# Early normalisation of images 1 to 3, softmax reciprocals by DMA a block later, and 5x5 convolutions without identity products

## The chip, the cores and the metric

The kernel runs on one core of one Trainium2 chip. The metric is the device time of one launch in microseconds (us). The core has five engines that run their own instruction streams in order: PE (TensorE, matrix products), DVE (VectorE), ACT (ScalarE), POOL (GpSimd) and SP (SyncE, which here does nothing but issue DMAs). An instruction waits on semaphores for what it needs, and everything behind it on the same engine waits with it.

## The reference, cut to what matters

Four layers, each with a residual, on `x` of shape (4, 128, 64, 64): four images of 128 channels and L = 4096 pixels. All is float32. `_gn` is a group norm over 4 channels at a time.

```
x = x + attention(_gn(x))     # q, k, v by 128x128 matrices; softmax over 4096 x 4096 scores
x = x + conv5x5(_gn(x))       # weights built from two small tables
x = x + scan(_gn(x))          # state-space scan, 64 states, forward and backward halves
x = x + conv3x3(_gn(x))
```

The scan's recurrence over 4096 pixels, for 128 channels and 64 states, is the largest piece of elementwise work; attention is the largest piece of products.

## The kernel before, in words

**The tiling.** Channels lie on the 128 partitions. A block of attention is 512 queries (`MM`), so an image has 8 blocks (`NM`), and a block has 32 units (`NJT`) of 128 keys. In unit `u`, PE makes a product of scores into PSUM, ACT takes its exponential into a ring of 8 slots, and two units later (`w = u - 2`) PE multiplies the slot by the values into the bank `acc`. The softmax denominators are sums over the keys. In image 0 they are added up beside, by DVE and POOL in turn, into two tiles (`side_sums`, L531 to L541). In images 1 to 3 PE makes them: once in four units, four products with a matrix of ones into the four column groups of bank `z` (`sums`, L511 to L524).

**The end of a block.** When the last unit of a block is through, `evict_sums` and `evict` copy sums and values out of PSUM (ACT). Then `attention` queues four steps for the units that follow (L624 to L625): `turn` one unit later (PE: small products that put the sums of 512 queries on partitions), `invert` two later (DVE: copy and reciprocal), `widen_out` four later (PE: `spread`, four 128-column products with the identity that lay the reciprocals along a row on all partitions), `settle` five later (DVE: multiply and add to the residual; ACT: a square for the next group norm).

**The 5x5 convolution** (`conv_pairs`, L837) treats rows in pairs, four chunks an image. In images 1 to 3 (`lean`) a chunk has three groups: a shared part of 10 products in bank `s`, copied to SBUF by ACT (`q`), and 15 products for the even and the odd rows (banks `a`, `z`), each closed with a product of the identity and `q` (L996), so that the shared part is added on PE. Image 0 has another grouping, which the change leaves as it is.

**The scan** is a loop of 1024 ticks (`scan_core`), 256 an image. A tick has one multiplication on POOL (`drive`, L1268), the decays on ACT (L1261), the recurrence on DVE (L1278), a multiplication on DVE (L1281) or POOL (`weigh`, L1299) as `to_pool` deals them out, and small products on PE (`collect`, L1317). SP loads one pair of broadcast rows (`br`, `cr`, L1239) in every second tick, four ticks ahead (`AHEAD`), into three buffers each.

**The order of the work** is written out by hand. All other work of the kernel is one generator, `images()`: `front(0)` to `front(3)` (attention, 5x5 convolution, then the operands of the scan), then the ends of all images (back projection, 3x3 convolution). Each `yield` names a price in estimated PE microseconds: 0.86 for a product (`PRODUCT`), 1.7 for a hop to another engine (`HOP`), 0.7 for a slot of the operands (`SLOT`). Image 0's front runs alone, ahead of the scan. From then on each tick of the scan earns 2.8 of credit (`PACE`; 1.5 in the last image, `ENDPACE`), and as much of the generator is issued between the tick's instructions as the credit pays for (L1583 to L1593). So the front of image b + 1 is spread over the 256 ticks of image b. If the scan's next image is due (four ticks ahead) and its first operands aren't there, `before` (L1567) issues the generator without ticks until they are.

**The operands** (`scan_operands`, L1034) are 60-odd slots of short steps on all engines. Beside them, image b + 1 begins: `start` (L1414) loads the image, `attention_start` (L396) takes its statistics (8 `bn_stats` on DVE, L401), makes the group norm (some 15 small DVE and POOL instructions, `group_norm`, L349), normalises on ACT (L392) and makes the values.

Of the kernel before, what the change touches and what calls it, by code (L numbers as in the profile page):

```python
# [24 lines left out]
F32 = mybir.dt.float32  # L25
I32 = mybir.dt.int32
AF = mybir.ActivationFunctionType
ALU = mybir.AluOpType
# [4 lines left out]
P = 128  # L33
GROUPS = 32
GN_EPS = 1e-5
CH = 1024
# [6 lines left out]

PRODUCT, HOP, SLOT, PACE, ENDPACE, AHEAD = 0.86, 1.7, 0.7, 2.8, 1.5, 4


BQ, BK, BX, BP, CONVB, BD, DSKIP, MAINB, CONVW, ALOG = 0, 1, 2, 3, 4, 5, 6, 7, 8, 12
# [3 lines left out]
def conv_preact_kernel(  # L53
# [340 lines left out]

    def attention_start(b, xn):

        st = stats_tile(f"a{b}")
        for i in range(NM):  # L400
            nc.vector.bn_stats(st[:, i, :], xn[:, bass.ts(i, MM)])  # L401
            yield 0.0
        gn = yield from group_norm(st, f"a{b}")
        while b > 0 and (b - 1, "taps") not in ready:
            yield 0.0
        v = pools["big"].tile([P, VSIZE], F32, tag="V", name=f"v_{b}")
        v = v[:, : NJT * C].rearrange("p (j c) -> p j c", c=C)
        pvs = {}

        def piece(i):  # L410
            cut = bass.ts(i, L // 4)
            normalise(xn[:, cut], xn[:, cut], gn)

        def keys(i):

            tag = "saz"[i % 3] if b == 0 else "s" if i < 3 else ("s", "s2")[i % 2]
            pvs[i] = bank(tag, f"pv_{b}_{i}").rearrange("p (t c) -> p t c", c=C)
            for t in range(TPM):
                nc.tensor.matmul(
                    pvs[i][:, t, :], xn[:, bass.ts(i * TPM + t, P)], wv, start=True, stop=True  # L420
                )

        def take(i):
            nc.scalar.copy(v[:, i * TPM : (i + 1) * TPM, :], pvs.pop(i))

        piece(0)
        yield SLOT
        for i in range(NM):
            if i % 2 == 0 and i // 2 + 1 < 4:
                piece(i // 2 + 1)  # L430
            keys(i)
            yield SLOT
            if b > 0:
                take(i)
                yield 0.0
            elif i > 0:
                take(i - 1)
        if b == 0:
            take(NM - 1)
        return xn, v  # L440

    def attention(b, xs, xn, v, st, safe, loads):
# [15 lines left out]
        def row_max(blk):  # L458

            part = small.tile([P, TPM, NM], F32, tag="part", name=f"part_{b}_{blk}")  # L460
            for t in range(TPM):
                for k in range(NM):
                    pp = bank("s", f"pmax_{b}_{blk}_{t}_{k}")
                    nc.tensor.matmul(
                        pp, rq[blk][:, bass.ts(t, P)], xn[:, bass.ts(k, MM)],
                        start=True, stop=True,
                    )
                    nc.vector.tensor_reduce(part[:, t, k : k + 1], pp, AX.X, ALU.max)
            m = small.tile([P, TPM], F32, tag="rmax", name=f"rmax_{b}_{blk}")
            nc.vector.tensor_reduce(m, part, AX.X, ALU.max)  # L470
            pb = bank("s", f"pmb_{b}_{blk}")
            spread(pb, m)
            mb[blk] = pools["bg"].tile([P, MM], F32, tag="w", bufs=4, name=f"mb_{b}_{blk}")
            nc.scalar.copy(mb[blk], pb)

        def spread(dst, cols):
# [66 lines left out]
        def evict_sums(blk):  # L543
            zs = None
            if not fill:
                zs = pools["bg"].tile([P, MM], F32, tag="zs", bufs=1, name=f"zs_{b}_{blk}")
                nc.scalar.copy(zs, zp.pop(blk))
            state[blk] = None, zs

        def evict(blk):  # L550
            raw = pools["bg"].tile([P, MM], F32, tag="raw", bufs=1, name=f"raw_{b}_{blk}")
            nc.scalar.copy(raw, acc.pop(blk))  # L552
            state[blk] = raw, state[blk][1]

# [43 lines left out]
        for u in range(N):  # L598
# [11 lines left out]
            if w >= 0:  # L610
                if w < N - HELD:
                    values(w)
                    cost += PRODUCT
                d = w % NJT
                if fill:
                    side_sums(w)
                elif d == NJT - 1:
                    sums(w)
                    cost += PRODUCT
                elif d % 4 == 3:  # L620
                    due.append((w, u + (3 if d == 3 else 1), u + NRING - 5))
                if d == NJT - 1:
                    evict_sums(blk - 1)
                    evict(blk - 1)  # L624
                    for n, f in ((1, turn), (2, invert), (4, widen_out), (5, settle)):  # L625
                        after(u, n, f, blk - 1)
            for f, args in later.pop(u, ()):
                f(*args)
                cost += PRODUCT if f in (turn, widen_out) else 0.0
            next(loads, None)  # L630
            yield cost or HOP
        for w in (N - 2, N - 1) if fill else ():
# [9 lines left out]
                nc.sync.dma_start(to[:, : part.shape[1], :], part)  # L642

        values(N - 4)
        yield PRODUCT
        while due:
            sums(due.pop(0)[0])
            yield PRODUCT
        for n in range(NRING - 4):
            taps_to(n)  # L650
        if not fill:
# [183 lines left out]
    def conv_pairs(b, xs, tag, st, st2, lean):  # L835
# [86 lines left out]
        piece(1)  # L922
        differences(0)
        K5 = 5
        steps, done = [], None
        taps5 = more[0] if wide else exchange(b)[:, : NTAP * C].rearrange("p (k c) -> p k c", c=C)

        def matrix(w, dx):
# [11 lines left out]
            )  # L940
            st2.squares(i, chunk(xs, c, y), xs[:, 0:1])

        for c in range(L // CH):
            j = c * CK
            if c < 2:
                piece(2 + c)
            if c < 3:
                differences(c + 1)
            accs = [
                (bank("s", f"pq_{b}_{c}"), ((SUM12, image, 2 * j + 2), (SUM34, image, 2 * j + 4))),  # L950
                (bank("a", f"pe0_{b}_{c}"),
                 ((0, image, 2 * j), (1, diff, j), (3, diff, j + 1))),
                (bank("z", f"pe1_{b}_{c}"),
                 ((0, image, 2 * j + 1), (2, diff, NP + j + 1), (4, diff, NP + j + 2))),
            ]
            if wide:
                total, first, last = (combo(n) for n in range(3))
                accs = [
                    (accs[0][0], (accs[0][1][1], (HSUM, total, j))),
                    (bank("y", f"pm_{b}_{c}"), ((HDIF, diff, j),)),  # L960
                    (accs[1][0], ((0, first, j), (3, diff, j + 1))),
                    (accs[2][0], ((2, last, j), (4, diff, NP + j + 2))),
                ]
            for n, (acc, parts) in enumerate(accs):
                k, total = 0, len(parts) * K5
                for w, view, r in parts:
                    for dx in range(K5):
                        k += 1
                        nc.tensor.matmul(  # L969
                            flat(acc), matrix(w, dx), view(r, dx),  # L970
                            start=k == 1, stop=k == total and (n == 0 or not lean),
                        )
                        if k == 3 and done is not None:
                            done()
                            done = None
                        if k % 3 == 0:
                            yield 3 * PRODUCT
                if n == 0:
                    qs = pools["bg"].tile([P, MM], F32, tag="w", bufs=4, name=f"q_{b}_{c}")

                    def done(acc=acc, qs=qs, c=c):
                        nc.scalar.copy(qs, acc)
                        for y in range(0 if lean else 2):
                            nc.gpsimd.tensor_tensor(
                                chunk(xs, c, y), chunk(xs, c, y), flat(qs), ALU.add
                            )
                    yield PRODUCT
                elif wide and n == 1:
                    def done(acc=acc, c=c):
                        for y, op in enumerate((ALU.subtract, ALU.add)):  # L990
                            nc.vector.tensor_tensor(
                                chunk(xs, c, y), chunk(xs, c, y), flat(acc), op
                            )
                else:
                    if lean:
                        nc.tensor.matmul(acc, ident, qs, start=False, stop=True)  # L996
                        yield PRODUCT

                    def done(acc=acc, c=c, y=n - len(accs) + 2):
                        add(c, y, acc)  # L1000
        yield HOP
# [399 lines left out]
    def program(safe):  # L1401
# [4 lines left out]
        if safe:  # L1406
            nc.sync.dma_start(cs[:, :10, :], kept_sums)

        def load(tile, b):
            for c in range(NCH):  # L1410
                nc.sync.dma_start(tile[:, bass.ts(c, CH)], xf[b][:, bass.ts(c, CH)])
                yield 0.0

        def start(b, after=0):  # L1414
# [3 lines left out]
            for _ in range(after):  # L1418
                yield 0.0
            xn = large(b, f"x_{b}")[:, :L]  # L1420
            yield from load(xn, b)
            for _ in range(after):
                yield 0.0
            return (yield from attention_start(b, xn))
# [1 line left out]
        def front(b, xn, v):  # L1426

            xs = large(b + 1, f"xs_{b}")[:, :L]
            st = Sums(f"e{b}")
            yield from attention(b, xs, xn, v, st, safe, load(xs, b))  # L1430
            st2 = Sums(f"s{b}")

            yield from conv_pairs(b, xs, f"A{b % 2}", st, st2, b > 0 or safe)
# [86 lines left out]
        with ExitStack() as es, tc.manual_schedule():  # L1520
# [26 lines left out]
            if not safe:  # L1547
                with tc.tile_pool(name="fill", bufs=2) as pools["fill"]:
# [7 lines left out]
                    with tc.tile_pool(name="tables", bufs=1) as tmp:  # L1556
                        for _ in chain(scan_constants(), build_conv_weights(tmp, more[0]), more_weights(*more)):
                            for _ in range(4):
                                next(work)
                    while (0, "convolved") not in ready:  # L1560
                        next(work)
                del pools["fill"]
# [112 lines left out]
```

## Time and profile before

| | |
|---|---|
| median of 3 runs | 4425.56 us (4419.15 to 4431.18) |
| the profiled execution's own time | 4426.94 us |
| its span, first to last instruction | 4425.1 us |
| PE busy, instructions | 3896.3 us (88%), 13352 |
| DVE busy | 3702.6 us (84%), 3471 |
| POOL busy | 3603.6 us (81%), 1713 |
| ACT busy | 2377.4 us (54%), 4301 |
| mean granted PE clock | 0.936 |
| DMA | 726.05 MB, mean 164 GB/s |

The shares are means over unlike stages. Up to 684 us image 0's front runs alone; then the scan's ticks run to 4355 us, in the first three images with the next image's front between them, in the last with the ends of the images. So every stage has its own bound, and is read by itself.

### The profile page before, as it was taken

The numbers are of one execution on the slowest core, as the hardware profiler recorded it, in microseconds if no ns is written. First come the engines' busy times: TensorE is split into PE (matmuls) and PEld (weight loads), VectorE is DVE, ScalarE is ACT, GpSimd is POOL, SyncE is SP. The second block draws the span as 40 slices with busy tenths as digits, with TensorE's granted clock in tenths as the row PEclk, the third lists the DMA queues.
The fourth block names the chain that finished last, engine by engine and source line by source line (L and its number), as shares of the span: only waits on it lengthen the run. The fifth ranks groups of instructions, "written<-read, shape, count | busy, mean of one in ns | idle before, by whom it ended". The sixth has DMA issues, their size and how long they took to land. (4 is left out here: it accounts for less than half of the span.)

```text
span 4425.1 us, 42907 instructions
## 1 busy us (share of the span) xinstructions
PE 3896.3 (88%) x13352; PEld 1486.0 (34%) x13352; DVE 3702.6 (84%) x3471; ACT 2377.4 (54%) x4301; POOL 3603.6 (81%) x1713
## 2 busy tenths in 40 slices
PE   8999997999999979999989889999989657575667
PEld 4444433333333323333333333333333112121212
DVE  4722217999999989999999889999999899999996
ACT  3333217666665376666664576666643754444533
POOL 3433307999999968999989889999999789999995
PEclk9999999999999989999999989999999868787888
DMA  1000016545555565544545564555555666656562
GB/s 64 21 1 1 0 53 231 185 167 176 177 176 182 176 238 198 176 176 168 185 173 181 201 228 168 175 177 175 176 181 177 223 221 206 228 195 232 187 227 84
DMA packets 216302, 726.05 MB, mean 164 GB/s; under 512 B 26240, under 2 KB 27520, under 8 KB 215808
## 3 DMA queue, kind: packets, MB, share of 16 engines
q1 hardware_dynamic: 214144, 722.49, 47.1%
q8 instruction: 107, 1.75, 0.2%
q14 instruction: 131, 1.07, 0.1%
q10 hardware_dynamic: 1920, 0.73, 0.1%
HBM read 653.98 MB, written 69.14 MB: 163 GB/s over the span
## 5 line engine op out<-in xcount | busy, mean ns | idle before, releaser
L1268 POOL TENSOR_TENSOR db<-dx,br 128x1024 f32<-128x1024 f32 x1024 | 2399.5, 2366 | 224.8 <-DMA dx<-dxd 76.7
L1261 ACT ACTIVATE da<-de,a_neg 128x512 f32<-128x512 f32 (+1 forms) x1640 | 1303.1, 797 | 759.6 <-DVE da L1278 305.0
L487 PE MATMUL sc<-r,x 128*128 128x512 f32 x2048 | 1082.2, 611 | 22.5 <-ACT last L1294 9.7
L499 PE MATMUL acc<-exchange,v 128*128 128x512 f32 x2048 | 1048.6, 594 | 2.7 <-ACT raw L552 0.5
L1299 POOL TENSOR_TENSOR hc<-hc,cr 128x1024 f32<-128x1024 f32 x386 | 913.3, 2366 | 22.9 <-ACT last L1294 20.9
L1281 DVE TENSOR_TENSOR hc<-da,cr 128x512 f32<-128x512 f32 (+1 forms) x1003 | 839.5, 837 | 65.7 <-issue 1.3
L1278 DVE TENSOR_TENSOR_SCAN da<-da,last,db 128x512 f32<-128x512 f32 (+1 forms) x480 | 863.1, 1798 | 22.6 <-POOL db L1268 17.7
L493 ACT ACTIVATE exchange<-sc 128x512 f32<-128x512 f32 x1024 | 603.6, 589 | 503.1 <-PE sc L487 494.6
L1317 PE MATMUL y<-hc,sel 128*32 128x512 f32 x4096 | 604.8, 650 | 284.4 <-POOL hc L1299 230.9
L487 PEld LDWEIGHTS sc<-r,x 128*128 128x128 f32 x2048 | 361.8, 190 | 596.5 <-issue 376.7
L499 PEld LDWEIGHTS acc<-exchange,v 128*128 128x128 f32 x2048 | 386.9, 190 | 500.6 <-issue 478.5
L1278 DVE TENSOR_TENSOR_SCAN hc<-da,last,db 128x512 f32<-128x512 f32 (+1 forms) x288 | 490.9, 1705 | 6.4 <-ACT da L1261 3.3
L1278 DVE TENSOR_TENSOR_SCAN da<-da,da,db 128x512 f32<-128x512 f32 x365 | 469.7, 1287 | 6.8 <-ACT da L1261 6.6
L541 POOL TENSOR_TENSOR sidep<-sidep,exchange 128x512 f32<-128x512 f32 x120 | 170.8, 1423 | 273.4 <-ACT exchange L493 271.1
L1317 PEld LDWEIGHTS y<-hc,sel 128*32 128x32 f32 x4096 | 114.4, 113 | 715.5 <-POOL hc L1299 315.2
L1278 DVE TENSOR_TENSOR_SCAN hc<-da,hc,db 128x512 f32<-128x512 f32 x251 | 322.0, 1283 | 32.7 <-ACT da L1261 8.9
L541 DVE TENSOR_TENSOR sided<-sided,exchange 128x512 f32<-128x512 f32 x120 | 95.9, 799 | 221.7 <-ACT exchange L493 220.3
L1278 DVE TENSOR_TENSOR_SCAN da<-da,db 128x512 f32<-128x512 f32 (+1 forms) x158 | 232.4, 1471 | 13.1 <-ACT da L1261 10.1
L703 PE MATMUL pcm<-xpm,cs 128*128 128x512 f32 x432 | 214.5, 646 | 25.2 <-ACT xpm L392 25.2
L969 PE MATMUL pe<-df,exchange 128*128 128x512 f32 x480 | 214.2, 595 | 0.0
L521 PE MATMUL zp<-exchange,ones 128*32 128x512 f32 x1536 | 205.3, 601 | 9.6 <-DVE xs L588 9.5
L1294 ACT COPY last<-da 128x1 f32<-128x1 f32 x474 | 73.8, 156 | 259.7 <-DVE hc L1281 257.2
(239 smaller groups left out, 2838.8 us busy)
## 6 DMA issues: line engine op xcount, KB each, us to landing
br<-bm SPq DMA_DIRECT2D x512, 512.0 KB, 5.2
cr<-cm SPq DMA_DIRECT2D x512, 512.0 KB, 4.0
de<-dd SPq DMA_DIRECT2D x64, 512.0 KB, 4.9
dx<-dxd SPq DMA_DIRECT2D x64, 512.0 KB, 6.2
x<-in_x_dram SPq DMA_DIRECT2D x16, 512.0 KB, 6.0
xs<-in_x_dram SPq DMA_DIRECT2D x16, 512.0 KB, 6.6
xsd<-xs SPq DMA_DIRECT2D x16, 512.0 KB, 6.8
xcd<-xc SPq DMA_DIRECT2D x16, 512.0 KB, 2.9
```

What stands on the lines that cost most here:

```text
L487: nc.tensor.matmul(sc, xn[:, bass.ts(j, P)], rq[blk], start=True, stop=True)
L493: nc.scalar.activation(pt, sc, AF.Exp)
L499: nc.tensor.matmul(acc[blk], v[:, j, :], ring[:, u % NRING, :], start=j == 0, stop=j == NJT - 1)
L541: eng.tensor_tensor(s, s, ring[:, u % NRING, :], ALU.add)
L703: nc.tensor.matmul(acc.rearrange("p (r w) -> p r w", w=W), weights[:, t, :], xp[:, y : y + RPM, dx : dx + W], start=t == 0, stop=t == k * ...
L969: nc.tensor.matmul(flat(acc), matrix(w, dx), view(r, dx), start=k == 1, stop=k == total and (n == 0 or not lean),)
L1261: nc.scalar.activation(da, rep["de", b, c, d, g][:, bass.ts(h, size)], AF.Exp, scale=a_neg[:, at(i)])
L1268: nc.gpsimd.tensor_tensor(dbs[i], rep["dx", b, c, d, g], rows["b", b, c, d, q], ALU.mult)
L1278: nc.vector.tensor_tensor_scan(h, da, db[:, cut], before, ALU.mult, ALU.add)
L1281: nc.vector.tensor_tensor(hc[:, cut], h, rows["c", b, c, d, q][:, cut], ALU.mult)
L1299: nc.gpsimd.tensor_tensor(hcs[i], hcs[i], rows["c", b, c, d, q], ALU.mult)
L1317: nc.tensor.matmul(y[r : r + SG, :], sel, hcs[first + gg][:, bass.ts(h, MM)], start=False, stop=q == NQ - 1, tile_position=(0, r), skip_gr ...
```

## The change

Four things change.

1. `normalise_ahead` runs in image 0's front, after the weights of the convolutions are built: it loads images 1 to 3, takes their statistics, normalises them and stores them to DRAM (`normed`). `start` then loads the normalised image, and `attention_start` makes no statistics, group norm or normalisation for images 1 to 3. The residual is still loaded from `x`.
2. `turn`, `invert`, `widen_out` go, but for the last block of an image. In their place, `spill` stores the sums to DRAM (2 units after the block), `gather` loads them with the queries on partitions (4), `invert_rows` adds the parts and takes the reciprocal on DVE (7), `put_rows` stores it (9) and `fetch_rows` loads it as a row on all partitions (11). At the end of the *next* block ACT copies that row into bank `z` (`stage_rows`), and `settle` follows a unit later. In image 0, two products with ones add up the side sums over the partitions first.
3. In the `lean` convolution ACT copies the shared part from its PSUM bank to a second one (`part`), and both groups of 15 go on adding to it in place. The products with the identity go. The order is shared part of chunk c, odd rows of chunk c - 1, even rows of chunk c; the shared parts alternate between banks `s` and `z`.
4. `PACE` is 2.74.

```diff
-PRODUCT, HOP, SLOT, PACE, ENDPACE, AHEAD = 0.86, 1.7, 0.7, 2.8, 1.5, 4
+PRODUCT, HOP, SLOT, PACE, ENDPACE, AHEAD = 0.86, 1.7, 0.7, 2.74, 1.5, 4
...
+    def normalise_ahead(pool):
+        for b in range(1, B):
+            t = pool.tile([P, L], F32, tag="ahead", name=f"ahead_{b}")
+            for c in range(NCH):
+                nc.sync.dma_start(t[:, bass.ts(c, CH)], xf[b][:, bass.ts(c, CH)])
+            st = stats_tile(f"a{b}")
+            for i in range(NM):
+                if i % 4 == 0:
+                    yield HOP
+                nc.vector.bn_stats(st[:, i, :], t[:, bass.ts(i, MM)])
+            yield HOP
+            gn = yield from group_norm(st, f"a{b}")
+            for c in range(NCH):
+                cut = bass.ts(c, CH)
+                normalise(t[:, cut], t[:, cut], gn)
+                nc.sync.dma_start(normed[b][:, cut], t[:, cut])
+                yield HOP
...
+            elif blk + 1 < NM:
+                zs = pools["bg"].tile([P, MM], F32, tag="zs", bufs=1, name=f"zs_{b}_{blk}")
+                pz = bank("z", f"pz_{b}_{blk}")
+                for g, e in enumerate("dp"):
+                    nc.tensor.matmul(
+                        pz[g * 32 : (g + 1) * 32, :], ones[:, :32], sides.pop((blk, e)),
+                        start=True, stop=True, tile_position=(0, g * 32), skip_group_check=True,
+                    )
+                nc.scalar.copy(zs[:64], pz[:64])
...
+        def spill(blk):
+            nc.sync.dma_start(zd[:n], zs[0 : n * 32 : 32, :])
...
+        def gather(blk):
+            nc.sync.dma_start(zt[:, :n, :], zd.rearrange("g (p j) -> p g j", j=RUN))
...
+        def invert_rows(blk):
+            nc.vector.tensor_reduce(z, zt.rearrange("p g j -> p j g"), AX.X, ALU.add)
+            nc.vector.reciprocal(zr, z)
...
+        def put_rows(blk):
+            nc.sync.dma_start(zd, zr)
...
+        def fetch_rows(blk):
+            row = zd.rearrange("p j -> (p j)").unsqueeze(0)
+            nc.sync.dma_start(rb, row.to_broadcast([P, MM]))
...
+        def stage_rows(blk, tag):
+            pb = bank(tag, f"rz_{b}_{blk}")
+            nc.scalar.copy(pb, rb)
...
-                    for n, f in ((1, turn), (2, invert), (4, widen_out), (5, settle)):
+                    for n, f in (
+                        (2, spill), (4, gather), (7, invert_rows), (9, put_rows), (11, fetch_rows)
+                    ):
                         after(u, n, f, blk - 1)
+                    if blk > 1:
+                        stage_rows(blk - 2, "z")
+                        after(u, 1, settle, blk - 2)
...
+        for c in range(NCK + 1 if lean else 0):
+            if c < NCK:
+                advance(c)
+                yield from shared_of(c)
+                done = lambda c=c: part(c)
+            if c > 0:
+                yield from second_of(c - 1)
+            else:
+                yield HOP
+                done()
+                done = None
+            if c < NCK:
+                yield from first_of(c)
...
+                    with tc.tile_pool(name="norm", bufs=1) as tmp:
+                        for _ in normalise_ahead(tmp):
+                            for _ in range(3):
+                                next(work)
```

`shared_of` is the group of 10 products, `second_of` and `first_of` those of 15, opened without clearing the bank; `part(c)` is `nc.scalar.copy(owns[c], held[c])`. A step given as `done` is issued after the third product of the group that follows.

## The prediction

> **What bounds the kernel now.** I read the page's totals first, then the busy times by stage, then the groups of instructions, then who waits for whom. The totals do not decide: three engines are over 80% busy.
>
> ```profile
> span 4425.1 us, 42907 instructions
> PE 3896.3 (88%) x13352; PEld 1486.0 (34%) x13352; DVE 3702.6 (84%) x3471; ACT 2377.4 (54%) x4301; POOL 3603.6 (81%) x1713
> ```
>
> So I cut the span at the stages that the groups' first and last starts show. Columns: window; its length and PE's busy time; then PEld, DVE, ACT, POOL, each with a count; granted PE clock; DMA share; GB/s.
>
> ```profile
> 30.00:500.00 470.00, 468.16 (x1233) 217.53 (x1232) 182.80 (x234) 167.67 (x286) 176.34 (x131) 1.00 0.01 5
> 730.00:1364.00 634.00, 621.54 (x2377) 232.96 (x2377) 602.68 (x618) 413.04 (x851) 598.62 (x259) 1.00 0.52 180
> 1380.00:1554.00 174.00, 173.95 (x543) 68.77 (x544) 163.46 (x101) 72.10 (x81) 168.76 (x78) 0.98 0.51 171
> 1554.00:1661.00 107.00, 78.29 (x313) 30.41 (x311) 87.96 (x114) 83.78 (x138) 73.36 (x39) 0.86 0.67 235
> 1600.00:1610.00 10.00, 10.00 (x40) 3.13 (x38) 6.94 (x11) 8.71 (x15) 0.00 (x0) 1.00 0.38 147
> 1630.00:1650.00 20.00, 14.89 (x80) 9.78 (x80) 17.67 (x20) 19.91 (x34) 15.27 (x7) 0.91 0.77 254
> 3540.00:4351.00 811.00, 514.92 (x1587) 153.79 (x1591) 779.84 (x461) 382.29 (x605) 769.09 (x350) 0.78 0.62 213
> ```
>
> The reader is to see: image 0's attention (30 to 500) is PE's alone. Image 1's attention (730 to 1364) is PE at 98%, with DVE at 95% and POOL at 94% close behind. Its convolution (1380 to 1554) is PE at 100%, POOL at 97%, DVE at 94%. In the operands (1554 to 1661) no engine is full on the mean, ACT is for a while (19.91 of 20), and POOL stands still for 10 us. Images 2 and 3 repeat this (attention 639 and 638 us). The last image (from 3540) is DVE's and POOL's.
>
> ```profile
> L401 DVE BATCH_NORM_STATS2 st_a<-x 128x6 f32<-128x512 f32 x32 | 20.6, 682 | 7.1 <-DMA x<-in_x_dram 7.1
> L392 ACT ACTIVATE x<-x,nb_a,rs_a 128x1024 f32<-128x1024 f32 x16 | 19.8, 1241 | 1.8 <-POOL nb_a L387 1.8
> L996 PE MATMUL pe<-q,ident 128*128 128x512 f32 x48 | 25.1, 605 | 0.0
> L479 PE MATMUL pzb<-ident,zr 128*128 128x128 f32 x256 | 33.9, 275 | 1.6 <-DVE zr L575 1.6
> L564 PE MATMUL pz<-zsel,zs 128*128 128x1 f32 x192 | 22.8, 240 | 0.0
> L521 PE MATMUL zp<-exchange,ones 128*32 128x512 f32 x1536 | 205.3, 601 | 9.6 <-DVE xs L588 9.5
> ```
>
> PE's ends are modelled and overlap, so I price products by the distance of starts. In the timeline of a block's end:
>
> ```profile
> 1903.66 0.95 PE L564 MATMUL pz<-zsel,zs 128*128 128x1 f32 x8
> ...
> 1904.54 1.92 PE L1317 MATMUL y<-hc,sel 128*32 128x512 f32 x16
> ...
> 1911.65 1.05 PE L479 MATMUL pzb<-ident,zr 128*128 128x128 f32 x8
> ...
> 1912.54 1.02 PE L487 MATMUL sc<-r,x 128*128 128x512 f32 x2
> ```
>
> A turn takes 0.88 us of PE, a widening 0.89, a 512-column product 0.86 (two passes of 0.43). SP's own waits name what it stands for:
>
> ```profile
> SPq L1239 <- POOL hc L1299: 1463.1, 342, 19.1
> SPq L1239 <- DVE hc L1281: 841.1, 277, 10.6
> ```
>
> SP is idle most of the time, waiting for a row buffer to come free.
>
> **What the Trainium skill says.** (1) Perfetto Trace Analysis, "Identifying the Most-Contended Engine": matmul busy time says little of how near TensorE is to its best. The trace agrees that it flatters (0.95 busy for 0.88 of time), so I count starts. (2) TensorEngine Tiling (Array Packing), "Key Properties": tiles of the array work independently. The trace agrees: four 32-column products of L521 fill 0.99 us (1900.44 to 1901.43), hardly more than one whole product. (3) The same page, "Instruction Overhead": a product with one column costs as much as one with 60. The trace agrees in kind: the 16 passes of one column with which image 0 turns its sums take 1.7 us (88.52 to 90.22). (4) DMA: Bandwidth & Descriptors, "Two DMAs through the same engine are not ordered": a DMA that reads what another wrote has to be held until the first one's semaphore. Before, SP shows few such waits (three for `dxd`, 4.3 us in all); the change adds two a block.
>
> **The change part by part.** The sum is made against the profiled execution's own 4426.94 us (its span plus 1.8 us around it), 1.4 us above the median of the runs.
>
> *Image 0's end of block.* Its turn costs 88.44 to 90.22 = 1.78 us, its widening 0.89 (95.46 to 96.35); 7 blocks x 2.67 = 18.7 us of PE go. Two products with ones come, in two column groups: at most two whole products, 1.72, at least one, 0.86; by L521 I take 1.0, so 7.0. The sums are now copied out ahead of the values: the ones' product ends 1.0 after the block, two ACT copies of 0.59 and their hand-over follow, and PE wants the bank `acc` again after a 0.86 score product: some 0.65 us of wait x 7 = 4.5. The POOL sum that the ones' product waits for follows its exponential at once and is about 2 us early. Net -7.
>
> *Normalising ahead.* DVE 24 statistics (16 us), three group norms (10), ACT 12 x 1.24 = 15, POOL 6 small ones, SP 12 loads and 12 stores. They fall in 30 to 500, where DVE is 39%, ACT 36%, POOL 38% and DMA 1% busy. What is queued behind: DVE's side sums and ACT's exponentials. A load waits on SP for the store of the image before, so DVE may stand up to 5 us; the ring of 8 slots gives PE 6 units of 1.72 = 10 us. I take +1 (0 to +6). If the cover failed, PE would wait for exponentials. Stage in sum: -6 (-14 to 0).
>
> *Attention of images 1 to 3.* 7 x (0.88 + 0.89) = 12.4 us of PE go per image. PE also no longer waits for `settle` to free bank `z`: 9.5/3 = 3.2. So up to -15.6. But DVE's work here stays (603 us: a reduction and a reciprocal for a copy and a reciprocal), and with 619 us in place of 634 it would be 97% busy; the best stretches of the page's slices have 98%. I take -11 (-4 to -15.6). Ticks don't change in number: credit of attention before 592 products x 0.86 + 1.7 = 511, /2.8 = 182; after, without 14 of them, 499/2.74 = 182.
>
> *Convolution.* 8 identity products x 0.86 = 6.9 us of PE go per image. ACT's copy stays a copy (PSUM to PSUM instead of SBUF), 15 products ahead of its first user. In credit the convolution loses 4 x 2.58 - 1.7 = 8.6. With attention's 12.0 and the 1.7 of the hop in the group norm that is 22.3. By the ticks' starts the operands of image 1 begin at tick 248, 248 x 2.8 = 694; after, 672/2.74 = tick 245.3. They are due at tick 252 and need 34 slots x 0.7 + 2 hops = 27 of credit, so before 17 are issued without ticks, after 9: the stretch in which POOL stands still (1600 to 1610) is halved, and this is how POOL, at 97% in the convolution, can profit. I take -7 (-3 to -10).
>
> *Operands.* Gone from beside them, for each of images 1 to 3: DVE 8 x 0.65 = 5.2 and some 3.3 of group norm, ACT 4 x 1.24 = 5.0, POOL two small ones. In 1630 to 1650 ACT is full, and four normalisations are in it or next to it. The load has the same size. I take -5 (-2 to -9).
>
> *The DMAs by SP.* Per block four small DMAs and one of 256 KB written on chip, all on SP's queue, behind which the row loads stand, and behind those POOL's `drive`. Issue is about 0.5 us each. Spill waits for ACT's copy; gather for spill's landing (the 128 KB store of `ys` lands in 3.1 us), two units, 5 us, later; invert on DVE for gather, 7.5 us after; put for invert; fetch for put's landing. Rows have room: the `br` issued at 1906.24 is used at 1918.29; the median of issue to use is 10.9 us in that stretch, of landing 5.2, so 5.7 to spare. SP comes to a load about 6 us before DVE comes to the same place in the program, so it will stand for put and gather some 2 to 4 us, within the room. ACT's staging copy adds 0.59 per block where ACT is 65% busy. I take +1.5 per image (0 to +6).
>
> *Sum.* -6 + 3 x (-11 - 7 - 5 + 1.5) = -6 - 64.5 = -70.5; 4426.9 - 70.5 = **4356 us**. The last image, 811 us, is untouched.
>
> **The rivals.**
>
> *A: DVE and POOL become the bound at once.* For: 95% and 94% in attention, 97% in the convolution. Against: both reach 96 to 98% in the last image. Attention -4, convolution -2, operands -5, DMAs +1.5: -6 - 3 x 9.5 = -34.5, 4392.
>
> *B: SP's queue, slower.* Two holds a block, gather behind spill and fetch behind put. It decides when a hold is longer than the 5.7 us of room: then POOL waits for rows and DVE for POOL. At 8 us a hold that is 2 x 2.3 = 4.6 us a block, 21 blocks: +97 on -70.5, 4453. Against: stores land in 3 us and the steps are 5 us apart. A late gather would stop DVE itself in `invert_rows`, at the same sort of price.
>
> *C: the operand stretch shrinks more than I price.* If the standstill goes and ACT's relief counts fully: -9 in the operands, -10 in the convolution, attention -13: -7 - 3 x 30.5 = -99, 4328.
>
> *D: that it doesn't do what it says* would be a normalisation that lands too late for `start`; image 1 is read at about 650, stored by about 350. I give it nothing.
>
> **How the numbers follow.** Forecast 0.61, A 0.22, B 0.07, C 0.10. About 0.3% (13 us) is what a measurement of this kernel can tell from no change. A's spread reaches into that with 0.04, B is slower: faster 0.89, same 0.04, slower 0.07. The outer bounds are 4427 - 14 - 3 x 34.6 = 4309 and, with all the least gains and 6 us for SP, 4427 - 3 x 3 = 4418. The range 4318 to 4402 leaves out B and the tails of A and C, 2 in 10.
>
> **What would show it.** Right: PE at most 97 to 98% in attention, DVE over 96%, attention some 623 us per image; turn and widening once an image only; L996 gone; POOL never idle for a whole 10 us between images; operands begun near tick 245. Wrong: attention still near 634 (A); POOL's wait for `br` or `cr` at several us a block, or DVE waiting for the gathered sums (B); PE below 99% in 230 to 400 (the cover of the normalisations).

## The result and the profile after

The changed kernel takes 4397.66 us (median of 4 runs, 4394.30 to 4400.41) against 4425.59 in the same job: a ratio of 0.9937, 95% interval 0.9926 to 0.9949. That is faster by 28 us, where 70 were forecast. The direction and the range held; the size was off by more than a factor of two.

The page of the changed kernel, the same two lines:

```profile
span 4396.1 us, 42164 instructions
PE 3829.8 (87%) x12828; PEld 1415.9 (32%) x12828; DVE 3698.7 (84%) x3465; ACT 2384.6 (54%) x4331; POOL 3601.9 (82%) x1712
```

PE lost 66 us of busy time. DVE's total is the same, but part of it has moved out of the ticks. The stages of the changed kernel, columns as before (length and PE, PEld, DVE, ACT, POOL, clock, DMA share, GB/s): image 0's attention, the attention of images 1 to 3, image 1's convolution, its operands, and the last image from 3540 on:

```profile
30.00:490.00 460.00, 458.77 (x1087) 198.43 (x1086) 202.71 (x285) 186.42 (x312) 180.51 (x137) 1.00 0.11 37
720.00:1350.00 630.00, 613.08 (x2275) 220.67 (x2274) 603.76 (x622) 415.38 (x858) 600.81 (x262) 1.00 0.55 186
1638.00:2275.00 637.00, 621.41 (x2292) 221.79 (x2291) 605.02 (x621) 415.94 (x860) 594.48 (x256) 0.99 0.54 182
2562.00:3200.00 638.00, 618.85 (x2292) 221.85 (x2291) 606.75 (x627) 415.25 (x861) 597.86 (x261) 0.99 0.54 181
1366.00:1531.00 165.00, 164.34 (x512) 64.64 (x510) 155.41 (x96) 67.91 (x77) 161.11 (x74) 0.99 0.50 171
1531.00:1637.00 106.00, 78.36 (x328) 29.47 (x326) 88.92 (x102) 80.61 (x136) 81.65 (x41) 0.92 0.68 243
3540.00:4322.00 782.00, 492.39 (x1548) 148.40 (x1548) 752.80 (x442) 373.37 (x591) 748.89 (x341) 0.79 0.60 208
```

Read PE and DVE against the length. In the three attentions PE has 5 to 10 us less to do than before, and most of that came back as PE waiting: 97.3, 97.6 and 97.0% against 98.0 to 98.6. DVE did not fill up; it stands at 95.8, 95.0 and 95.1%, as before. The attentions are hardly shorter.

The groups show that the change does what it says:

```profile
L546 PE MATMUL zp<-exchange,ones 128*32 128x512 f32 x1536 | 205.8, 600 | 0.1
L664 DVE TENSOR_TENSOR rz<-raw,rz 128x512 f32<-128x512 f32 x28 | 19.2, 686 | 25.9 <-ACT rz L624 25.7
L411 DVE BATCH_NORM_STATS2 st_a<-ahead 128x6 f32<-128x512 f32 x24 | 15.0, 679 | 0.4 <-DMA ahead<-in_x_dram 0.3
L392 ACT ACTIVATE ahead<-ahead,nb_a,rs_a 128x1024 f32<-128x1024 f32 x12 | 14.8, 1230 | 0.0
L504 PE MATMUL pzb<-ident,zr 128*128 128x128 f32 x32 | 6.3, 361 | 0.1
L641 PE MATMUL pz<-zsel,zs 128*128 128x1 f32 x24 | 4.8, 321 | 8.2 <-ACT zs L572 8.2
```

The widening (L504) is down from 256 passes to 32 and the turn of images 1 to 3 (L641) from 192 to 24; the wait of the sums for `settle` (9.6 us before) is 0.1.

**Where the time came from**, by the first starts of stages in the two traces (us):

| | before | after |
|---|---|---|
| first tick of the scan | 683.8 | 677.4 |
| attention, first score to last value product, images 1, 2, 3 | 639.7, 642.7, 640.8 | 633.1, 638.8, 641.3 |
| convolution, first to last product | 174.6, 173.9, 174.3 | 166.0, 167.7, 165.8 |
| operands of the next image begin at tick | 248, 502, 758 | 245, 498, 752 |
| ticks 0 to 255, to 511, to 767, to 1023 | 945.1, 937.0, 938.0, 846.6 | 931.0, 938.3, 948.6, 827.1 |

Image 0's front is 6.4 us shorter. All ticks together are 21.8 us shorter (3666.8 to 3645.0), and not where the forecast had it: the third image's ticks take longer. The ticks of the first three images in one stretch, then those of the last image, in the kernel before:

```profile
683.80:3503.90 2820.10, 2664.68 (x9861) 1010.01 (x9860) 2617.99 (x2591) 1737.26 (x3263) 2566.84 (x1157) 0.97 0.53 185
3503.90:4350.60 846.70, 528.58 (x1629) 156.38 (x1626) 812.23 (x488) 403.74 (x643) 801.35 (x363) 0.78 0.62 214
```

And in the changed one:

```profile
677.40:3495.30 2817.90, 2620.60 (x9489) 961.37 (x9487) 2612.42 (x2559) 1737.97 (x3291) 2572.04 (x1154) 0.97 0.56 190
3495.30:4322.50 827.20, 514.27 (x1616) 152.82 (x1616) 797.11 (x466) 393.90 (x624) 790.24 (x359) 0.78 0.61 212
```

In the first three images PE has 44 us less to do and DVE 5.6, and the time is 2.2 us shorter. In the last image, which the forecast called untouched, DVE has 15 us less (and PE 14), and the time is 19.5 us shorter. The operands of the last image begin at tick 752 instead of 758, so fewer of their steps are left when its own ticks begin. As far as two traces can say, the time does not follow the work taken off PE.

**The count of ticks is part of every stage's time.** The same windows, with only the instructions on the tile `db` (DVE's recurrences, then POOL's one multiplication per tick), the kernel before and then the changed one:

```profile
730.00:1364.00 634.00, 458.70 (x365) 430.26 (x185) 1.00 0.52 180
1380.00:1554.00 174.00, 119.97 (x53) 121.43 (x53) 0.98 0.51 171
```

```profile
720.00:1350.00 630.00, 458.46 (x365) 431.21 (x184) 1.00 0.55 186
1366.00:1531.00 165.00, 114.45 (x50) 116.93 (x50) 0.99 0.50 171
```

The convolution is 9 us shorter and holds 3 ticks less: 3.28 us a tick before, 3.30 after. The number of ticks per image is fixed, so those three ticks run somewhere else. The shorter stage by itself is no gain. The attentions show the same. Counted from first score to last value product, the three hold 552 ticks in 1923.2 us before and 550 in 1913.2 us after: 3.48 us a tick in both kernels.

### The profile page after: what moved, and what is told of

It reads as the page before. It is cut to its first block, busy times and chain, and to the rows that moved or that the text cites. A ratio compares the mean times of both kernels' runs of the same rounds, so it can differ in the third digit from the quotient of the medians.

```text
span 4396.1 us, 42164 instructions
## 1 busy us (share of the span) xinstructions
PE 3829.8 (87%) x12828; PEld 1415.9 (32%) x12828; DVE 3698.7 (84%) x3465; ACT 2384.6 (54%) x4331; POOL 3601.9 (82%) x1712
## 5 line engine op out<-in xcount | busy, mean ns | idle before, releaser
L1039 PE MATMUL pq<-xpe,cs 128*128 128x512 f32 x280 | 134.5, 631 | 39.8 <-ACT xpe L392 39.8
```

## The experiments

Ratios are to the kernel before, measured beside each run, with 95% intervals; the changed kernel has 0.9937.

**The three parts alone.** Each has its own credit, and what the credit alone does to the time (7 to 17 us, at the end of this section) is in each of these differences. First the early normalisation (credit 2.8):

```diff
+    def normalise_ahead(pool):
...
-            yield from load(xn, b)
+            yield from load(xn, normed[b] if b > 0 else xf[b])
```

> The kernel before with the early normalisation alone (credit per tick stays 2.8). Theory D, DVE is the bound of all ticks, its hand-overs included, so the change gained what DVE work left the ticks (20.7 us between the two traces) plus image 0's front: about -19 us against the kernel before, 4406. Theory P, PE is the bound as predicted and the missing gain is lost elsewhere: -14 (the 3 x 5 of the operands, +1 in image 0), 4411. Theory S, the softmax DMAs through SP's queue ate some 40 us: also -14 here.

4401.57 us, 0.9944 (0.9930 to 0.9957): -24, more than any theory gave it. Then the softmax part:

```diff
-PRODUCT, HOP, SLOT, PACE, ENDPACE, AHEAD = 0.86, 1.7, 0.7, 2.8, 1.5, 4
+PRODUCT, HOP, SLOT, PACE, ENDPACE, AHEAD = 0.86, 1.7, 0.7, 2.75, 1.5, 4
...
-                    for n, f in ((1, turn), (2, invert), (4, widen_out), (5, settle)):
+                    for n, f in (
+                        (2, spill), (4, gather), (7, invert_rows), (9, put_rows), (11, fetch_rows)
+                    ):
```

> The kernel before with the softmax reciprocals by DMA alone (credit per tick 2.75, so that the work fills as many ticks). D: only image 0's front gains, -7 us, and nothing or up to -4 in the ticks: 4415 to 4419. P: -7 and 3 x (-11 + 1.5): -35, 4390. S: slower than before by 10 us or more, since the queue's cost is all here.

4417.23 us, 0.9983 (0.9975 to 0.9990): -8, with the first tick at 675.0 instead of 683.8. So what this part gains for sure is image 0's front, and neither PE's 12 us per attention nor a cost of SP's queue shows in the total. Theory S (10 us slower or more) and P (35 us faster) are both missed by more than a shift of the credit was seen to do; D's 4415 to 4419 holds. Then the convolution:

```diff
-PRODUCT, HOP, SLOT, PACE, ENDPACE, AHEAD = 0.86, 1.7, 0.7, 2.8, 1.5, 4
+PRODUCT, HOP, SLOT, PACE, ENDPACE, AHEAD = 0.86, 1.7, 0.7, 2.77, 1.5, 4
...
-                    if lean:
-                        nc.tensor.matmul(acc, ident, qs, start=False, stop=True)
-                        yield PRODUCT
...
+        def part(c):
+            owns[c] = bank("a", f"pe0_{b}_{c}")
+            nc.scalar.copy(owns[c], held[c])
```

> The kernel before with the convolution without identity products alone (credit per tick 2.77). D: nothing, within 4 us of before, though PE has 24 products (21 us) less and the convolution looks shorter, because it holds fewer ticks. P: -21 us, 4404. S: -21 us too.

4426.75 us, 1.0001 (0.9992 to 1.0009): nothing, at this credit, as D had it; P and S had 21 us. Its first convolution in the profile, all instructions:

```profile
1392.00:1557.00 165.00, 164.34 (x516) 64.74 (x520) 152.70 (x95) 67.20 (x75) 160.75 (x74) 0.99 0.49 169
```

It is as short as in the changed kernel, and POOL is as full (97%) as in the kernel before; it holds 49 ticks, at 3.37 us.

**The prices of PE and DVE**, by adding work to the changed kernel without touching the credit, so that the order of all instructions stays:

```diff
             scores(u)
             cost += PRODUCT
+            if b > 0 and j in (5, 21):
+                extra = small.tile([P, 6], F32, tag="extra", name=f"extra_{b}_{u}")
+                nc.vector.bn_stats(extra, xn[:, bass.ts(blk, MM)])
```

> The changed kernel with 48 additional statistics instructions of 0.65 to 0.68 us on DVE, 16 in each attention of images 1 to 3, whose results nobody reads; 32 us of DVE work. D: +27 to +33 us on the changed kernel's 4398: about 4428. P: DVE has room beside PE, at most +8. S: at most +8.

4418.34 us, 0.9987 (0.9980 to 0.9993): 0.0050 above the changed kernel, 22 us for 32.6 us of added DVE work. P and S (at most 8) fall, and D's 27 to 33 is not reached.

```diff
-            nc.tensor.matmul(sc, xn[:, bass.ts(j, P)], rq[blk], start=True, stop=True)
+            for _ in range(2 if b > 0 and j in (5, 21) else 1):
+                nc.tensor.matmul(sc, xn[:, bass.ts(j, P)], rq[blk], start=True, stop=True)
```

> The changed kernel with 48 score products of images 1 to 3 made twice (the second overwrites the first with the same values), 16 per attention: 48 x 0.86 = 41 us of PE work. D, DVE is the bound of the ticks: at most +8 us on the changed kernel's 4398. P, PE is the bound: +35 to +41, 4435.

4409.70 us, 0.9955 (0.9941 to 0.9968): 0.0018 above the changed kernel, 8 us for 41 us of PE work, and the intervals overlap, so that anything from nothing to 16 us fits. The attentions of the two runs, DVE's first, then PE's:

```profile
718.00:1361.00 643.00, 619.76 (x2284) 222.38 (x2281) 614.48 (x639) 415.72 (x859) 602.98 (x262) 0.99 0.53 183
1647.00:2292.00 645.00, 624.97 (x2294) 221.36 (x2294) 615.59 (x640) 416.83 (x860) 596.30 (x258) 0.99 0.53 180
2572.00:3218.00 646.00, 623.31 (x2294) 222.42 (x2295) 617.44 (x645) 416.74 (x863) 601.95 (x262) 0.99 0.53 180
```

```profile
718.00:1357.00 639.00, 629.57 (x2315) 229.37 (x2312) 605.91 (x623) 417.44 (x859) 602.94 (x263) 0.99 0.54 185
1642.00:2286.00 644.00, 633.22 (x2326) 228.74 (x2326) 607.22 (x625) 417.85 (x860) 596.09 (x260) 1.00 0.53 180
2567.00:3217.00 650.00, 635.95 (x2327) 230.39 (x2328) 609.63 (x629) 419.76 (x863) 602.15 (x262) 0.99 0.53 180
```

DVE's share does not rise when it is given more: 95.6, 95.4, 95.6%. The stage gets longer instead. By the starts of the stages, 32.6 us of DVE cost 21 us of attention and 41 us of PE cost 20. So D, in which DVE alone is the bound, holds only in part, and P with its 35 to 41 fails; a microsecond of DVE costs about two thirds of one, a microsecond of PE a half in the stage and a fifth in the total. Nor is POOL free:

```diff
-                    else n % 2 == 0 if "operands" in ready else n % 2 == 1
+                    else n % 2 == 0 if "operands" in ready else i % 7 in (1, 3, 5)
```

> The changed kernel with POOL taking 3 of 7 of the multiplications by the C rows instead of 2 of 5 in the narrow ticks outside the operands (some 550 ticks): about 16 multiplications move, 22 us of DVE work go and 37 us of POOL work come, where POOL has 98 us of waits over the three attentions. D: -8 to -20 us, 4378 to 4390. P: within 4 us of the changed kernel, since PE is the bound.

4395.54 us, 0.9917 (0.9904 to 0.9931). In the trace DVE has 20.8 us less and POOL 37.6 more in the ticks, and the ticks are 5.9 us shorter. That is the direction of D, less than its range by the medians and at its lower end by the ratios; the interval just overlaps that of the changed kernel.

**What the early normalisation gains.** It was given back piece by piece, first DVE's statistics:

```diff
+        if b > 0:
+            st = stats_tile(f"a{b}")
+            for i in range(NM):
+                nc.vector.bn_stats(st[:, i, :], xn[:, bass.ts(i, MM)])
+                yield 0.0
```

> The early normalisation alone, but with the 24 statistics instructions of images 1 to 3 left on DVE where they stood (their results unread, 16 us); group norm and normalisation stay away. D, the gain is DVE work taken out of the ticks: of the 24 us that the part alone gained 10 to 16 go, 4412 to 4418. Theory N, the gain is ACT's normalisations and the shorter chain of the operands: it stays, 4402 to 4405.

4401.00 us, 0.9938 (0.9925 to 0.9950): the gain stays. D's account of it falls. Then ACT's work:

```diff
             if b == 0:
                 normalise(xn[:, cut], xn[:, cut], gn)
+            else:
+                nc.scalar.activation(xn[:, cut], xn[:, cut], AF.Identity)
```

> The early normalisation alone, but with 12 activations of 1024 columns on ACT where the normalisations stood, which copy the image onto itself (15 us). D: at most 5 us of the 24 go, 4402 to 4407. N: 10 to 20 go, 4412 or more, since ACT is full there and the values wait for it.

4405.17 us, 0.9949 (0.9936 to 0.9961): it stays again, so N falls as well. Then the statistics with the whole group norm:

```diff
+        if b > 0:
+            st = stats_tile(f"a{b}")
+            for i in range(NM):
+                nc.vector.bn_stats(st[:, i, :], xn[:, bass.ts(i, MM)])
+                yield 0.0
+            yield from group_norm(st, f"a{b}")
```

> The early normalisation alone, but the statistics and the whole group norm (15 DVE steps, two POOL steps, its hop of 1.7 in the credit) run where they stood, their results unread; only ACT's normalisations stay away. Theory G, the chain of the group norm with the waits it puts on DVE and POOL was the gain: 15 us or more of the 24 go, 4415. Theory K, the hop in the credit was it, which lets the next operands begin a tick earlier: the same. Neither: it stays at 4401 to 4406, and it was the sum of them or the normalisations that waited for the group norm.

4430.63 us, 1.0011 (1.0005 to 1.0018): all of it is gone. And only the hop, in which no work is:

```diff
+        if b > 0:
+            yield HOP
```

> The early normalisation alone with nothing but the hop of 1.7 put back into the credit. K: 15 us or more of the 24 go. G: nothing goes, 4401.

4418.93 us, 0.9985 (0.9977 to 0.9993): 17 us of the 24 go with a number that is only bookkeeping. Between this run and the one before lie 12 us (0.9985 to 1.0011), 4 an image, with the statistics and the group norm. Since the statistics alone cost nothing, and these 12 are more than the whole early normalisation gains beside this run (0.0015, 7 us), they are no clean price of that work either.

**What goes with what.** Early normalisation and softmax part without the convolution, credit 2.75 (the diffs of the two parts), and the same with POOL's 3 of 7:

> Early normalisation and softmax reciprocals by DMA, convolution as before, credit 2.75 per tick. D: the parts' gains add up, -24 and -8, 4394, and the convolution's part is worth nothing: within 4 us of the changed kernel or better. P: 15 to 20 us slower than the changed kernel, since the identity products are back on PE.

4401.78 us, 0.9941 (0.9929 to 0.9953). The convolution is worth nothing here either (P had 15 to 20 us for it), but the parts don't add up: -26 where they alone gave -24 and -8. Beside the changed kernel at the same credit of 2.75 (0.9976, in the table below) this one, without the convolution's part, is even 15 us faster.

> As the run before, and POOL takes 3 of 7 of the multiplications. D: some 5 to 10 us less than without, 4385 to 4390, the best so far. P: no difference to the run before.

4389.59 us, 0.9911 (0.9898 to 0.9925): the fastest kernel of the study. Its interval lies just below the changed kernel's. It is 12 to 13 us below the run without, more than D's 5 to 10; P, which had no difference, falls.

**The credit alone.** Six kernels with no change but the number of credit per tick:

```diff
-PRODUCT, HOP, SLOT, PACE, ENDPACE, AHEAD = 0.86, 1.7, 0.7, 2.8, 1.5, 4
+PRODUCT, HOP, SLOT, PACE, ENDPACE, AHEAD = 0.86, 1.7, 0.7, 2.86, 1.5, 4
```

> The kernel before with 2.86 of credit per tick in place of 2.8, so that the operands begin some 5 ticks earlier and the stretch without ticks between images gets short. K: 10 to 25 us faster than before. G, and D with DVE as the bound of the ticks: within 5 us of before, since the same work is done in other ticks.

> The changed kernel with 2.68 of credit per tick in place of 2.74, so that the operands begin some 5 ticks later. K: 10 to 25 us slower than the changed kernel. D: within 5 us.

> The kernel before with 2.79 of credit per tick instead of 2.8: no work added or removed, the interleaving of work and ticks shifts by 0.4%. Theory F, the interleaving by itself is worth 5 to 15 us either way, and the numbers of the parts hold that much chance: 5 us or more from before. Theory X, only work counts: within 4 us.

> The same with 2.81. F: 5 us or more from before, up or down, not in line with 2.79 and 2.86. X: within 4 us.

> The changed kernel with 2.73 instead of 2.74. F: 5 us or more from the changed kernel. X: within 4 us.

> The changed kernel with 2.75 instead of 2.74. F: 5 us or more from the changed kernel. X: within 4 us.

| kernel, credit | median us | ratio | interval |
|---|---|---|---|
| before, 2.79 | 4420.98 | 0.9985 | 0.9978 to 0.9992 |
| before, 2.80 | 4425.59 | 1 | |
| before, 2.81 | 4414.13 | 0.9975 | 0.9966 to 0.9985 |
| before, 2.86 | 4439.81 | 1.0031 | 1.0019 to 1.0042 |
| changed, 2.68 | 4412.38 | 0.9969 | 0.9957 to 0.9980 |
| changed, 2.73 | 4407.74 | 0.9956 | 0.9943 to 0.9970 |
| changed, 2.74 | 4397.66 | 0.9937 | 0.9926 to 0.9949 |
| changed, 2.75 | 4415.00 | 0.9976 | 0.9967 to 0.9986 |

K falls: with 2.86 the kernel before is 14 us slower, where K had it 10 to 25 faster, though 2.68 made the changed kernel 14 us slower, as K said. F holds: a shift of the credit by 0.4%, with nothing added or removed, moves the time by 7 to 17 us, up or down, in no line with its size. A little work does change hands with the credit, since `to_pool` deals by stages: POOL takes 386 of the multiplications by the C rows at 2.80, 389 at 2.79 and 391 at 2.81, and 385 at 2.74, 389 at 2.73 and 388 at 2.75. That can't be the cause on both sides: of the three of each kernel, the kernel before is slowest, and the changed one fastest, where POOL has fewest.

2.80 is the slowest of its three, 2.74 the fastest of its three. The mean of the three is 0.9987 for the kernel before and 0.9956 for the changed one: 0.0031, 14 us. Three points a side scatter by 0.0013 and 0.0020, which gives this number a standard error of 6 us. The best estimate is that half of the 28 us is what the work gained, 6 to 9 of it in image 0's front, and that the rest is how the instructions fall between each other at 2.80 and at 2.74; how much exactly is not shown.

## Why the prediction was wrong, by its own steps

**Image 0's front** (-6): right. It measured -6.4. The first tick starts at 675.0 to 677.4 in each profile with the softmax part and at 683.8 to 685.9 in each without, and the normalisations cost too little to be told from the 2 us by which these starts scatter (684.7 in the run with them alone; 1 was taken). The cover held: PE is busy 458.77 of 460 us.

**Attention** (-11 an image): the step that failed. The reasoning was that PE is the bound and DVE, at 95%, has room up to 98%, "the best stretches of the page's slices". Measured: -6.6, -3.9 and +0.5, that is 10 us where 33 were forecast, and the three together hold two ticks less; the time of a tick, 3.48 us, did not change. So a microsecond taken off PE was not a microsecond of the stage. The sign named for rival A, attention still near 634, is what came. DVE's 95% was nearly full already. All of DVE's waits that the view lists in image 1's attention in the kernel before:

```profile
DVE da L1278 <- POOL db L1268: 6.4, 7, 1.6
DVE hc L1278 <- ACT da L1261: 2.7, 7, 0.7
DVE hc L1278 <- POOL db L1268: 0.7, 1, 0.7
DVE zall L573 <- PE pz L564: 0.5, 1, 0.5
DVE da L1278 <- ACT exchange L493: 0.4, 1, 0.4
```

They sum to 10.7 us, but DVE is idle for 634 - 602.7 = 31.3. The other 20 us lie in about 300 gaps of under 0.14 us between its 618 instructions. They are too short for the view of waits, and they don't go away: the changed kernel has 310 in 630 us, 21.6 us in all. The 98% comes from two stretches of 100 us in the last image (its mean is 96%), where one recurrence does 1024 columns and DVE has 461 instructions in 811 us. I compared a share of long instructions with one of short ones.

What PE was spared came back as waits. By the view of waits PE stands 35.6 us in the three attentions before and 58.0 after, though the 9.5 for `settle` are gone; 56.8 of the 58.0 are for ACT, against 24.4 before, and of these the waits for ACT's copy of `last` went from 9.6 to 20.5. That copy takes the end of a recurrence, and over the whole changed kernel ACT waits for DVE ahead of it:

```profile
L1416 ACT COPY last<-da 128x1 f32<-128x1 f32 x476 | 73.7, 155 | 275.1 <-DVE hc L1403 273.0
```

So PE, with less to do, stands behind ACT, and ACT behind DVE. Rival A was the better mechanism, and its 4392 the nearer number, though with 7 to 17 us in the credit alone that nearness is in part luck. A was not the whole: by the runs with added work a microsecond of PE still costs 0.2 to 0.5.

**Convolution** (-7): failed too. The stage is shorter by 6 to 9 us, as priced, and the operands begin at tick 245, as worked out. But the stage's own POOL share stayed at 97%, the tick's time did not change, and alone, at a credit of 2.77, the part is worth nothing (1.0001). I let the gain come out where ticks stand still between images. That stretch (start of tick 252 to 254) did shrink, from 32.5, 22.8 and 23.9 us to 20.5, 6.9 and 13.7; that is 38 us, with only 22 gained over all ticks. More credit shrinks it as well (9.2, 16.8, 6.9 at 2.86) and makes the kernel slower. That the steps which no longer run in the standstill run between ticks, and lengthen those, is the likely reason; no run isolates it.

**Operands** (-5): the size can't be settled by the total. With the credit as in the kernel before (the run with the hop put back) the whole early normalisation is worth 0.0015, 7 us or 2 an image, in its range of -2 to -9. The 4 us an image that stand beside the statistics and the group norm there are more than this whole, so none of these is better than to a few us.

**The DMAs by SP** (+1.5): right in kind. SP's own waits in its queue, the line for DVE's reciprocals first, then the two for the landing of a store (sum in us, times, longest):

```profile
SPq L611 <- DVE zr L605: 54.5, 10, 14.4
...
SPq L618 <- DMA zi<-zr: 35.4, 16, 5.4
...
SPq L597 <- DMA zd<-zs: 32.7, 16, 4.9
```

The waits for landing stay below the 5.7 us of room. POOL's waits for `br` in the three attentions did rise, from at most 0.2 us to 2.4, 8.9 and 4.9, but its waits for `dx` fell from 18.9, 13.3 and 11.6 to 7.4, 7.5 and 12.2, and the two together are 43.3 us after 44.0. The normalisations alone, without any of the new softmax DMAs, also have 4.3, 6.5 and 3.0 us on `br`. The largest of SP's new waits, 248.8 us of `spill` for ACT (L590), lies for 234.5 us in image 0's front, ahead of the scan, where no row load stands behind it. Rival B needed 4.6 us in each of 21 blocks. Since the softmax part alone is not slower, B is out.

**What the prediction lacked** is the table of credits: it treated the credit as a means to keep stages apart, and gave no room to the interleaving itself, worth up to 17 us for a shift of 0.4%. The exact reason for single values (why 2.74 is better than 2.73 and 2.75) was not found and stays open.

## What to carry to other kernels

Where three engines are over 90% busy, price a removed microsecond on each by adding one and measuring: in these attentions it was worth 0.7 on DVE and 0.2 (0 to 0.4) on PE in the total, not 1 on the busiest. Read an engine's room from its waits and not from its share alone, since short instructions leave gaps that don't go away. And where the order of work is paced by a number, measure each side at some neighbouring values of it, or a difference of half a per cent says little about the work.

## What was not expected of the hardware

- DVE at 95% busy with instructions of mostly 0.7 to 1.3 us was nearly full here: 31 us idle in 634, 11 of them in waits. Given 10.9 us more per attention it stayed at 95.4 to 95.6%.
- The same work, shifted by 0.4% of credit against the ticks, differs by up to 17 us in 4400; 3 to 5 of 1024 multiplications go from DVE to POOL with it, which does not explain both directions.
- 24 statistics (16 us) or 12 activations (15 us) put between the operands cost nothing that can be told from 0.9944 (0.9938 and 0.9949), while a hop of 1.7 in the credit per image, with no work in it, cost 17 us.
